# Cross attention with q, k and v of 512 tokens by seven products of quadrants, and a feature-major output

## The chip, the cores and the metric

The kernel runs on one core of one Trainium2 chip. A core has a matrix engine (TensorE, "PE" in the profile, with its weight loads shown apart as "PEld"), a vector engine (VectorE, "DVE"), a scalar engine (ScalarE, "ACT"), a general engine (GpSimd, "POOL") and a sync engine ("SP") that issues transfers. Matrix products are written to PSUM, eight banks of 128 partitions x 512 float32 values, and have to be copied from there to SBUF, the working memory of 128 partitions, before PE can use them again. The metric is the time of one execution on the device, in microseconds (us); smaller is better.

## What is computed

The program is a decoder of two layers with six sublayers; each adds its result to the tokens x (8 batches of 256 tokens, 512 features, float32) and normalizes. The change is in the fifth, the cross attention of the second layer. The context and the projected tokens themselves serve together as keys and values:

```python
q = jnp.einsum('bsd,ed->bse', x, wq)
k_new = jnp.einsum('bsd,ed->bse', x, wk)
v_new = jnp.einsum('bsd,ed->bse', x, wv)
k = jnp.concatenate([k_cache, k_new], axis=1)
v = jnp.concatenate([v_cache, v_new], axis=1)
scores = jnp.einsum('bqd,bkd->bqk', q, k) * (1.0 / math.sqrt(512))
attn = jax.nn.softmax(scores, axis=-1)
out = jnp.einsum('bqk,bkd->bqd', attn, v)
return jnp.einsum('bqd,ed->bqe', out, wo)
...
x = _layernorm(x + _L1_xattn_ref(x, mask, ctx_2048, ctx_2048, wq, wk, wv, wo), axis=-1)
```

k_cache and v_cache are both the context (256 tokens per batch), so each of the 256 queries of a batch has 512 keys, in one head of 512 features. The mask isn't applied by this function.

## The kernel before

The 2048 tokens are 16 tiles x[t] of 128 tokens (partitions) by 512 features. A group is 4 tiles, or 512 tokens, or two batches; there are NG = 4 groups. The contraction over 512 features is done in KB = 4 blocks of 128 partitions, so `project` (L192) issues four matmuls into one PSUM bank.

The stages around this one, self attention ahead of it and the routed attention behind it, have their order on PE, DVE, ACT and POOL written out by hand (`causal_attention`, `tc.manual_schedule`). The cross attention between them has not: the framework's scheduler takes the instructions in the order of the code as their priority, and puts a later one that is ready where an earlier one would wait. It also inserts all waits. A tile with `bufs=1` has a single buffer, and its next use waits until the last reader of the old one is done.

For each group (L1592 to L1605):

- SP issues the loads of the context token-major (`cx`, L1594) and feature-major (`ctxT`, L1596), 1 MB each, with two buffers each.
- `group_xT` turns the four tiles of x on PE (`transpose`, L185: four 128x128 transposes into one of two "tr" banks), and `evacuate` (L136) copies them to `xT`, in turn on ACT and DVE.
- `feature_major` (L1472) makes q and k with the features on partitions: for each of four feature blocks four matmuls of 512 columns into the one "mm" bank, then a copy. For q the copy multiplies by -1/sqrt(512) on ACT (L1482); for k it goes to ACT and DVE in turn.
- `token_major` (L1485) makes v with the tokens on partitions, in four such products.
- `Pipeline` (L269) runs three stages of each tile, shifted against each other: `scores` (matmuls of 256 columns against `ctxT` and against `kT`, a minimum on DVE, the exponential on ACT with the row sum, its reciprocal), `products` (the weights turned, 128 x 512 of attention output `po` in four matmuls, divided by the row sum on DVE into y, L1583) and `out_project` (L247: y turned, multiplied by wo, added to x and normalized; the normalization uses POOL for the reciprocal root, L164 and L165). `pipe.flush()` (L1599) finishes the tiles of the group before, between q and k.

The eight PSUM banks are: one for "mm" (products of q, k, v and output), two for transposes, two for `po`, three for scores (`attention_pools`, L1429). The weights wq, wk, wv, wo lie in `w_l1x`; they were loaded during the self attention, from 1301.3 to 1419.1 us.

Of the kernel before, what the change touches and what calls it, by code (L numbers as in the profile page):

```python
# [25 lines left out]
GT = TPG * P  # L30
KB = D // P
# [19 lines left out]
def decoder_kernel(ctx: ExitStack, tc: tile.TileContext, a: dict, out: bass.AP):  # L51
    nc = tc.nc
    xin = a["x"].rearrange("b s d -> (b s) d").rearrange("(t p) d -> p t d", p=P)
    cin = a["ctx_2048"].rearrange("b s d -> (b s) d").rearrange("(t p) d -> p t d", p=P)
# [3 lines left out]
    small = ctx.enter_context(tc.tile_pool(name="small", bufs=4))  # L58
# [5 lines left out]
    x = []  # L64
# [3 lines left out]
    def load_x(tiles):  # L68
# [13 lines left out]
        out=hide_b,  # L82
        in_=hide_b,
# [35 lines left out]
    ctx_d = dram.tile([P, KB, B * S], F32, tag="ctx_d", name="ctx_d")  # L119
# [16 lines left out]
    def evacuate(dst, src):  # L136

        flip[0] ^= 1
        if flip[0]:
            nc.scalar.copy(dst, src)  # L140
        else:
            nc.vector.tensor_copy(dst, src)
# [39 lines left out]
    def layernorm(dst, src):  # L182
        norm_later(dst, src)()

    def transpose(psum, dst, src):  # L185

        pt = psum.tile([P, KB, P], F32, tag="tr", name="pt")
        for k in range(KB):
            nc.tensor.transpose(pt[:, k, :], src[:, k * P : (k + 1) * P], ident)
        evacuate(dst, pt)  # L190

    def project(ps, lhsT, rhs, n=KB):  # L192

        for k in range(n):
            nc.tensor.matmul(ps, lhsT=lhsT(k), rhs=rhs(k), start=(k == 0), stop=(k == n - 1))  # L195
# [33 lines left out]

        return xT, [(0, [(TR, lambda ti=ti: step(ti))]) for ti in range(TPG)]  # L230

    def group_xT(work, psum, g):
        xT = work.tile([P, KB, GT], F32, tag="xT", name="xT", bufs=1)
        for ti in range(TPG):
            transpose(psum, xT[:, :, ti * P : (ti + 1) * P], x[g * TPG + ti])
        return xT
# [7 lines left out]
    def add_norm(work, t, ps):  # L244
        add_norm_later(work, t, ps)()

    def out_project(work, psum, t, y, w):  # L247

        yT = work.tile([P, KB, P], F32, tag="yT", name="yT")
        transpose(psum, yT, y)  # L250
        ps = psum.tile([P, D], F32, tag="mm", name="ps_o")
        project(ps, lambda k: yT[:, k, :], lambda k: w[:, k, :])
        add_norm(work, t, ps)

    def softmax_rows(ps, sc, nk, mn, sm):

        nc.vector.tensor_tensor_reduce(
            out=sc,
            in0=ps,
            in1=mask[:, 2 * P - nk :],  # L260
            scale=1.0,
            scalar=3.0e38,
            op0=ALU.add,
            op1=ALU.min,
            accum_out=mn,
        )
        nc.scalar.activation(sc, sc, AF.Exp, bias=mn, scale=-1.0, accum_out=sm)

    class Pipeline:  # L269

# [1155 lines left out]
                fill(9.0)  # L1426
                happen("end")

    def attention_pools(st, name):  # L1429
        work = st.enter_context(tc.tile_pool(name=f"{name}_work", bufs=2))  # L1430
        psum = st.enter_context(tc.tile_pool(name=f"{name}_ps", bufs=1, space=PSUM))
        ps_s = st.enter_context(tc.tile_pool(name=f"{name}_pss", bufs=3, space=PSUM))
        ps_t = st.enter_context(tc.tile_pool(name=f"{name}_pst", bufs=2, space=PSUM))

        class pools:
            @staticmethod
            def tile(shape, dt, tag, name):
                if tag == "tr":
                    return ps_t.tile(shape, dt, tag=tag, name=name)
                return psum.tile(shape, dt, tag=tag, name=name, bufs=2 if tag == "pv" else 1)  # L1440

        return work, pools, ps_s, ps_t
# [20 lines left out]
    def out_block(pools, yT, i, w, done):  # L1463
# [4 lines left out]
            lambda k: w[:, k, :],  # L1468
            done,
        )  # L1470

    def feature_major(work, pools, xT, w, at, tag, scale=None, bufs=2):  # L1472

        r = work.tile([P, KB, GT], F32, tag=tag, name=tag, bufs=bufs)
        for c in range(KB):
            cs = slice(at + c * P, at + (c + 1) * P)
            ps = pools.tile([P, GT], F32, tag="mm", name="ps_f")
            project(ps, lambda k: w[:, k, cs], lambda k: xT[:, k, :])
            if scale is None:
                evacuate(r[:, c, :], ps)  # L1480
            else:
                nc.scalar.mul(r[:, c, :], ps, scale)  # L1482
        return r

    def token_major(pools, xT, w, at, ti):  # L1485

        ps = pools.tile([P, D], F32, tag="mm", name="ps_t")
        project(
            ps, lambda k: xT[:, k, ti * P : (ti + 1) * P], lambda k: w[:, k, at : at + D]
        )  # L1490
        return ps

    def self_weights(w, behind):
        return load_w(w, 0, a["L1_attn_w_qkv"], 3 * D, behind), load_w(
# [55 lines left out]
    def cross_weights(w):  # L1550
# [2 lines left out]
            for i, n in enumerate(("wq", "wk", "wv", "wo"))  # L1553
        ]

    def cross_attention(wq, wk, wv, wo):
        def cross_step(work, pools, ps_s, g, ti, qT, kT, v, cx, ctxT):
            k0 = (ti // 2) * S
            sc = work.tile([P, 2 * S], F32, tag="sc", name="sc_x")
            sm = small.tile([P, 1], F32, tag="xsm", name="xsm")  # L1560

            def scores():
                ps = ps_s.tile([P, 2 * S], F32, tag="sc", name="ps_x")
                q = lambda k: qT[:, k, ti * P : (ti + 1) * P]
                project(ps[:, :S], q, lambda k: ctxT[:, k, k0 : k0 + S])
                project(ps[:, S:], q, lambda k: kT[:, k, k0 : k0 + S])
                mn = small.tile([P, 1], F32, tag="xmn", name="xmn")
                nc.vector.tensor_reduce(mn, ps, AX.X, ALU.min)
                nc.scalar.activation(sc, ps, AF.Exp, bias=mn, scale=-1.0, accum_out=sm)
                nc.vector.reciprocal(sm, sm)  # L1570

            def products():
                pT = work.tile([P, KB, P], F32, tag="pT", name="pT_x")
                transpose(pools, pT, sc)
                po = pools.tile([P, D], F32, tag="pv", name="po_x")
                t0 = (ti // 2) * 2
                project(
                    po,
                    lambda k: pT[:, k, :],
                    lambda k: cx[:, t0 + k, :] if k < 2 else v[:, t0 + k - 2, :],  # L1580
                )
                y = work.tile([P, D], F32, tag="row", name="y_x", bufs=3)
                nc.vector.tensor_scalar(y, po, sm, None, ALU.mult)  # L1583
                out.append(y)

            out = []
            return scores, products, lambda: out_project(work, pools, g * TPG + ti, out[0], wo)

        with ExitStack() as st:
            work, pools, ps_s, ps_t = attention_pools(st, "x")  # L1590
            pipe = Pipeline()
            for g in range(NG):  # L1592
                cx = work.tile([P, TPG, D], F32, tag="cx", name="cx_x")
# [10 lines left out]
                for ti in range(TPG):  # L1604
# [115 lines left out]
    with ExitStack() as st_self:  # L1720
# [6 lines left out]
        w = pool.tile([P, 2 * half], F32, tag="w", name="w_l1a")  # L1727
        with ExitStack() as st_blocks:
# [4 lines left out]
            ps_t = st_blocks.enter_context(tc.tile_pool(name="c_pst", bufs=2, space=PSUM))  # L1733
# [98 lines left out]
```

## Time and profile before

| what | value |
|---|---|
| median of 3 runs | 2313.8 us (2313.7 to 2317.38) |
| profiled execution | 2321.55 us, span 2319.8 us |
| PE busy over the span | 2148.9 us (93%) |
| DVE busy | 1194.6 us (51%) |
| POOL busy | 658.8 us (28%) |
| ACT busy | 424.1 us (18%) |
| cross attention, on PE | 1574.72 to 1951.72 us |

In the profile a row of a group gives the line, the engine, the operation, what it writes and reads by the program's names, shapes and count, then the busy time in us and the mean of one in ns, and then the idle time of the engine just before these instructions with what ended most of it. L195 is the line of the helper `project`; groups are therefore told apart by the tile that they write: `ps_f` is q and k, `ps_t` v, `ps_x` the scores, `po_x` the attention output, `ps_o` the output projection, `pt` a transpose. A row of the timeline gives start and length in us, then the same names; what stands in brackets is the idle time before it and what it waited for. Matmuls are pipelined and overlap, so their durations are longer than their distance from start to start.

### The profile page before, as it was taken

How to read it: one execution, taken by the hardware profiler on the slowest of the kernel's cores; microseconds unless marked ns; L12 is line 12 of the kernel's file. 1: busy time of each engine (PE TensorE's matmuls, PEld its weight loads, DVE VectorE, ACT ScalarE, POOL GpSimd, SP SyncE). 2: the span in 40 equal slices, each digit the busy share in tenths (PEclk: the TensorE clock that was granted, in tenths of full speed). 3: DMA queues.
4: the chain of work that ended last, by engine and by line, in shares of the span. 5: the costliest groups of instructions: out<-in, count | busy, mean ns of one | idle time of the engine just before them, and what ended most of it. 6: DMA issues, size and time to landing. Idle time of an engine off the chain costs nothing.

```text
span 2319.8 us, 35250 instructions
## 1 busy us (share of the span) xinstructions
PE 2148.9 (93%) x15064; PEld 1164.0 (50%) x15064; DVE 1194.6 (51%) x1847; ACT 424.1 (18%) x607; POOL 658.8 (28%) x768
## 2 busy tenths in 40 slices
PE   7799989888998998999969999999999999999996
PEld 4455555544444454555524455444554545555543
DVE  3566666657888963122224646451222213567667
ACT  1223233330000012211112222221111111112212
POOL 0344555455555723000022433230000000022223
PEclk9899999999999998999979999999999999999998
DMA  7899602305224143131140201003001000000000
GB/s 233 302 384 383 243 2 65 112 1 172 73 66 151 42 141 129 62 136 64 46 146 19 74 15 60 1 1 127 27 10 36 1 0 1 1 10 11 10 19 28
DMA packets 107851, 197.53 MB, mean 85 GB/s; under 512 B 6960, under 2 KB 26544, under 8 KB 107696
## 3 DMA queue, kind: packets, MB, share of 16 engines
q1 hardware_dynamic: 102576, 178.49, 22.1%
q0 software_dynamic: 5120, 16.78, 2.1%
q8 instruction: 121, 1.98, 0.3%
q14 instruction: 34, 0.28, 0.0%
HBM read 93.54 MB, written 112.20 MB: 89 GB/s over the span
## 4 chain that ended last, share of the span: by engine, by line
PE 40%; DVE 5%; POOL 2%; ACT 1%; issue 1%; DMA 1%; POOLq 0%; ACTq 0%; DVEq 0%
PE ps_f L206 7%; PE ps_t L206 6%; PE ps_f L195 5%; PE ps_t L195 2%; PE po_x L195 2%; PE ps_o L206 2%; PE ps_o L195 2%; PE ps_q L1203 2%; PE ps_x L195 2%; PE ps_k L1257 2%; PE ps_pv L1300 2%; PE ps_pv L1310 1%; DVE rsum L1318 1%; DVE neg L1210 1%; DVE bn_st L169 1%; PE ps_q L1193 1%
## 5 line engine op out<-in xcount | busy, mean ns | idle before, releaser
L1210 DVE TENSOR_REDUCE neg<-ps_q 128x12 f32<-128x1536 f32 x128 | 224.9, 1757 | 344.7 <-PE ps_q L1203 343.9
L195 PE MATMUL ps_y<-kv,wt 128*128 128x512 f32 x640 | 282.5, 600 | 5.5 <-POOL kv L563 3.8
L1275 POOL TENSOR_SCALAR_AFFINE_SELECT pT<-pT 128x1024 f32<-128x1024 f32 x128 | 140.1, 1095 | 514.3 <-ACT pT L1274 513.7
L1274 ACT ACTIVATE pT<-ps_k 128x1536 f32<-128x1536 f32 x128 | 185.6, 1450 | 539.1 <-PE ps_k L1266 517.4
L1318 DVE RECIPROCAL rsum<-ps_pv 128x256 f32<-128x256 f32 x128 | 224.1, 1751 | 42.1 <-PE ps_pv L1310 41.4
L195 PEld LDWEIGHTS ps_y<-kv,wt 128*128 128x128 f32 x640 | 120.8, 192 | 155.7 <-issue 137.5
L164 POOL TENSOR_SCALAR rstd<-bn_mv 128x1 f32<-128x1 f32 x80 | 16.6, 207 | 563.9 <-DVE bn_mv L170 559.9
L1285 POOL TENSOR_TENSOR pT<-pT 128x512 f32<-128x512 f32 x112 | 142.3, 1271 | 9.3
L195 PE MATMUL ps_f<-xT,w_l1x 128*128 128x512 f32 x256 | 120.1, 612 | 3.3 <-ACT qT L1482 2.1
L206 PE MATMUL ps_f<-xT,w_l1a 128*128 128x512 f32 x256 | 119.6, 611 | 3.0 <-ACT xT L219 3.0
L206 PE MATMUL ps_t<-w_l1f,xT 128*128 128x512 f32 x256 | 120.1, 607 | 0.3 <-DVE sel L1649 0.3
L1036 PE MATMUL po_m<-dn,hT 128*128 (+1 forms) x216 | 104.5, 622 | 11.8 <-ACT hT L1029 10.3
L1121 POOL DMA_INDIRECT w_l1x<-ys,slots x32 | 32.3, 1011 | 280.1 <-DMA ys<-y_m 272.3
L1310 PE MATMUL ps_pv<-pT,ones_v 128*32 128x256 f32 (+1 forms) x1152 | 86.2, 382 | 12.5 <-POOL pT L1285 10.4
L601 DVE TENSOR_REDUCE yc<-z 128x64 f32<-128x512 f32 x128 | 86.1, 674 | 6.2 <-issue 5.8
L1193 PEld LDWEIGHTS <-ident_b 128*128 128x128 bf16 x512 | 50.5, 99 | 75.7 <-issue 72.0
L1193 PE MATMUL ps_q<-hide_b,ident_b 128*128 128x256 bf16 x512 | 78.2, 276 | 9.7 <-ACT pT L1274 8.7
L195 PEld LDWEIGHTS ps_f<-xT,w_l1x 128*128 128x128 f32 x256 | 46.8, 193 | 62.3 <-issue 48.5
L1257 PE MATMUL ps_k<-qT,kz 32*128 32x256 f32 (+1 forms) x1024 | 69.5, 358 | 8.3 <-DVE neg L1210 6.7
L206 PEld LDWEIGHTS ps_f<-xT,w_l1a 128*128 128x128 f32 x256 | 46.9, 192 | 59.0 <-issue 54.2
L195 PE MATMUL pg<-gu,xT_b 128*128 x216 | 72.1, 470 | 1.4 <-ACT xT_b L219 1.4
L1018 DVE TENSOR_TENSOR h_b<-h_b,pg 128x352 f32<-128x352 f32 x36 | 18.8, 521 | 103.7 <-ACT h_b L1017 103.7
(304 smaller groups left out, 3511.6 us busy)
## 6 DMA issues: line engine op xcount, KB each, us to landing
xs<-zero SPq DMA_DIRECT2D x8, 4352.0 KB
ys<-zero SPq DMA_DIRECT2D x8, 4352.0 KB
filters<-in_L_xattn_k SPq DMA_DIRECT2D x4, 2560.0 KB
first_h<-xs SPq DMA_DIRECT2D x36, 256.0 KB
ys<-y_m SPq DMA_DIRECT2D x36, 256.0 KB
gu<-in_L_ffn_gate_up_proj SPq DMA_DIRECT2D x3, 2816.0 KB
wt<-filters SPq DMA_DIRECT2D x32, 256.0 KB
x<-in_x SPq DMA_DIRECT2D x16, 256.0 KB
```

The costliest lines, as they stand in the source:

```text
L195: nc.tensor.matmul(ps, lhsT=lhsT(k), rhs=rhs(k), start=(k == 0), stop=(k == n - 1))
L206: nc.tensor.matmul(ps[0], lhsT=lhsT(k), rhs=rhs(k), start=(k == 0), stop=(k == KB - 1))
L601: nc.vector.tensor_reduce(yc[:, lb], z, AX.X, ALU.add)
L1036: nc.tensor.matmul(po, lhsT=hT[:m, i, :], rhs=dn[i][:m, bass.ds(e, 1), :], start=(i == 0), stop=(i == len(FCH) - 1),)
L1193: nc.tensor.matmul(block[:, s, 0:3:2, :], lhsT=ident_b, rhs=hide_b.unsqueeze(1).broadcast_to([P, 2, P]), start=True, stop=False,)
L1210: nc.vector.tensor_reduce(neg[(u // upb) % 2][:, :, :, c].rearrange("p j s -> p s j"), block, AX.X, ALU.max, negate=True,)
L1257: nc.tensor.matmul(block[:, s, at, :], lhsT=k(rows, c, b * S + j * P, P), rhs=q(rows, c, b * S + j * P, P * (2 - j)), start=True, stop=False,)
L1274: nc.scalar.activation(p[:, 0:3].rearrange("p j s q -> p s j q"), block, AF.Exp)
L1275: nc.gpsimd.affine_select(out=p[:, 0:2].rearrange("p j s q -> p (j s) q"), in_=p[:, 0:2].rearrange("p j s q -> p (j s) q"), compare_op=ALU ...
L1285: nc.gpsimd.tensor_tensor(p[:, 3], p[:, 1], p[:, 2], ALU.add)
L1310: nc.tensor.matmul(ps[32 * s : 32 * s + 32, 1, j * P :], lhsT=ones_v, rhs=p[:, 1, s, :] if j else first[:, :, s, :], start=(j == 0), stop= ...
L1318: nc.vector.reciprocal(r, ps[:, 1, :])
```

## The change

It rewrites the cross attention; the other stages stay as they are.

- The three products of a group with wq, wk and wv are taken as products of 2 x 2 quadrants. `seven_weights` makes, once, three sums of quadrants of each weight matrix into new tiles and one in place (a21), on DVE for wq and on POOL for wk and wv. `seven_tokens` makes four differences of quadrants of `xT` per group, three on DVE and one on POOL. `seven_products` makes seven products of quadrants (each 256 x 256 x 256, in one bank), copies the first with ACT, and adds the others up on DVE straight from PSUM: seven additions, into the quadrants of q, k or v and into two partial sums u2 and u3 that have one buffer each, as p1 has.
- Scores are taken per batch (two tiles). The scale 1/sqrt(512) is no longer in q: it is in the exponential and, by a small DVE instruction, in the negated maximum.
- The attention output is computed with features on partitions, for a batch of 256 tokens at a time, so it needs no turning before the output projection. ACT copies it to `yT`. The division by the row sum moves into the residual: one `scalar_tensor_tensor` multiplies by the reciprocal and adds x.
- The context is loaded per batch (512 KB each), still with two buffers.
- PSUM is divided anew: four banks for "mm" (products, all transposes, output projection), two for `po`, two for scores. `xT`, `qT`, `kT`, `v`, `pT`, `yT` and the differences have one buffer each.
- Helpers that nothing else uses are removed; `transpose` gets the name of the bank's tag as a parameter.

```diff
+    def quadrants(m):
+
+        return [[m[:, 2 * j : 2 * j + 2, i * S : (i + 1) * S] for j in range(2)] for i in range(2)]
+
+    def seven_weights(work, w, eng):
+
+        (a11, a12), (a21, a22) = quadrants(w)
+        sums = [work.tile([P, 2, S], F32, tag="ws", name="ws", bufs=9) for _ in range(3)]
+        eng.tensor_tensor(sums[0], a21, a22, ALU.add)
+        eng.tensor_tensor(sums[1], sums[0], a11, ALU.subtract)
+        eng.tensor_tensor(sums[2], a12, sums[1], ALU.subtract)
+        eng.tensor_tensor(a21, a11, a21, ALU.subtract)
+        return a11, a12, sums[1], a21, a22, sums[0], sums[2]
+
+    def seven_tokens(work, xT):
+
+        (b11, b21), (b12, b22) = quadrants(xT)
+        t = work.tile([P, 4, 2, S], F32, tag="ts", name="ts", bufs=1)
+        nc.vector.tensor_tensor(t[:, 0], b12, b11, ALU.subtract)
+        nc.gpsimd.tensor_tensor(t[:, 2], b22, b12, ALU.subtract)
+        nc.vector.tensor_tensor(t[:, 1], b22, t[:, 0], ALU.subtract)
+        nc.vector.tensor_tensor(t[:, 3], b21, t[:, 1], ALU.subtract)
+        return b11, b21, t[:, 1], t[:, 2], t[:, 3], t[:, 0], b22
+
+    def seven_products(work, pools, weights, tokens, dst, token_major=False):
+
+
+
+        def product(n):
+            ps = pools.tile([P, 2, S], F32, tag="mm", name="ps_7")
+            rows, cols = (tokens, weights) if token_major else (weights, tokens)
+            for i in range(2):
+                project(
+                    ps[:, i, :],
+                    lambda k: rows[n][:, k, i * P : (i + 1) * P],
+                    lambda k: cols[n][:, k, :],
+                    n=2,
+                )
+            return ps
+
+        def part(name):
+            return work.tile([P, 2, S], F32, tag=name, name=name, bufs=1)
+
+        p1, u2, u3 = part("p1"), part("u2"), part("u3")
+        add = lambda out, ps, other: nc.vector.tensor_tensor(out, ps, other, ALU.add)
+        nc.scalar.copy(p1, product(0))
+        add(dst(0, 0), product(1), p1)
+        add(u2, product(2), p1)
+        add(u3, product(3), u2)
+        add(dst(1, 0), product(4), u3)
+        ps = product(5)
+        add(dst(1, 1), ps, u3)
+        add(u2, ps, u2)
+        add(dst(0, 1), product(6), u2)
+
     def cross_attention(wq, wk, wv, wo):
-        def cross_step(work, pools, ps_s, g, ti, qT, kT, v, cx, ctxT):
-            k0 = (ti // 2) * S
-            sc = work.tile([P, 2 * S], F32, tag="sc", name="sc_x")
-            sm = small.tile([P, 1], F32, tag="xsm", name="xsm")
+        scale = D**-0.5
+
+        def batch(work, pools, ps_s, n, qT, kT, v, cx, ctxT):
+
+            q0 = n % 2 * S
+            sc, sm = [], []
 
             def scores():
-                ps = ps_s.tile([P, 2 * S], F32, tag="sc", name="ps_x")
-                q = lambda k: qT[:, k, ti * P : (ti + 1) * P]
-                project(ps[:, :S], q, lambda k: ctxT[:, k, k0 : k0 + S])
-                project(ps[:, S:], q, lambda k: kT[:, k, k0 : k0 + S])
-                mn = small.tile([P, 1], F32, tag="xmn", name="xmn")
-                nc.vector.tensor_reduce(mn, ps, AX.X, ALU.min)
-                nc.scalar.activation(sc, ps, AF.Exp, bias=mn, scale=-1.0, accum_out=sm)
-                nc.vector.reciprocal(sm, sm)
+                for i in range(2):
+                    ps = ps_s.tile([P, 2 * S], F32, tag="sc", name="ps_x")
+                    q = lambda k: qT[:, k, q0 + i * P : q0 + (i + 1) * P]
+                    project(ps[:, :S], q, lambda k: ctxT[:, k, :])
+                    project(ps[:, S:], q, lambda k: kT[:, k, q0 : q0 + S])
+                    mx = small.tile([P, 1], F32, tag="xmx", name="xmx")
+                    nc.vector.tensor_reduce(mx, ps, AX.X, ALU.max, negate=True)
+                    nc.vector.tensor_scalar(mx, mx, scale, None, ALU.mult)
+                    sc.append(work.tile([P, 2 * S], F32, tag="sc", name="sc_x"))
+                    sm.append(small.tile([P, 1], F32, tag="xsm", name="xsm"))
+                    nc.scalar.activation(sc[i], ps, AF.Exp, bias=mx, scale=scale, accum_out=sm[i])
+                    nc.vector.reciprocal(sm[i], sm[i])
 
             def products():
-                pT = work.tile([P, KB, P], F32, tag="pT", name="pT_x")
-                transpose(pools, pT, sc)
-                po = pools.tile([P, D], F32, tag="pv", name="po_x")
-                t0 = (ti // 2) * 2
-                project(
-                    po,
-                    lambda k: pT[:, k, :],
-                    lambda k: cx[:, t0 + k, :] if k < 2 else v[:, t0 + k - 2, :],
-                )
-                y = work.tile([P, D], F32, tag="row", name="y_x", bufs=3)
-                nc.vector.tensor_scalar(y, po, sm, None, ALU.mult)
-                out.append(y)
-
-            out = []
-            return scores, products, lambda: out_project(work, pools, g * TPG + ti, out[0], wo)
+                pT = work.tile([P, KB, S], F32, tag="pT", name="pT_x", bufs=1)
+                for i in range(2):
+                    transpose(pools, pT[:, :, i * P : (i + 1) * P], sc[i], "mm")
+                yT.append(work.tile([P, KB, S], F32, tag="yT", name="yT_x", bufs=1))
+                for f in range(0, KB, 2):
+                    po = pools.tile([P, 2, S], F32, tag="pv", name="po_x", bufs=2)
+                    for i in range(2):
+                        cols = slice((f + i) * P, (f + i + 1) * P)
+                        project(
+                            po[:, i, :],
+                            lambda k: cx[:, k, cols] if k < 2 else v[:, q0 // P + k - 2, cols],
+                            lambda k: pT[:, k, :],
+                        )
+                    nc.scalar.copy(yT[0][:, f : f + 2, :], po)
+
+            def out():
+                for i in range(2):
+                    ps = pools.tile([P, D], F32, tag="mm", name="ps_o")
+                    project(
+                        ps, lambda k: yT[0][:, k, i * P : (i + 1) * P], lambda k: wo[:, k, :]
+                    )
+
+                    t = 2 * n + i
+                    r = work.tile([P, D], F32, tag="row", name="res")
+                    nc.vector.scalar_tensor_tensor(r, ps, sm[i], x[t], ALU.mult, ALU.add)
+                    layernorm(x[t], r)
+
+            yT = []
+            return scores, products, out
 
         with ExitStack() as st:
-            work, pools, ps_s, ps_t = attention_pools(st, "x")
+            work = st.enter_context(tc.tile_pool(name="x_work", bufs=2))
+            pools = st.enter_context(tc.tile_pool(name="x_ps", bufs=4, space=PSUM))
+            ps_s = st.enter_context(tc.tile_pool(name="x_pss", bufs=2, space=PSUM))
+            wq7 = seven_weights(work, wq, nc.vector)
+            wk7 = seven_weights(work, wk, nc.gpsimd)
+            wv7 = seven_weights(work, wv, nc.gpsimd)
             pipe = Pipeline()
             for g in range(NG):
-                cx = work.tile([P, TPG, D], F32, tag="cx", name="cx_x")
-                nc.sync.dma_start(out=cx, in_=cin[:, g * TPG : (g + 1) * TPG, :])
-                ctxT = work.tile([P, KB, GT], F32, tag="ctxT", name="ctxT_x")
-                nc.sync.dma_start(out=ctxT, in_=ctx_d[:, :, g * GT : (g + 1) * GT])
-                xT = group_xT(work, pools, g)
-                qT = feature_major(work, pools, xT, wq, 0, "qT", -(D**-0.5))
+                ctxs = []
+                for n in range(2 * g, 2 * g + 2):
+                    cx = work.tile([P, 2, D], F32, tag="cx", name="cx_x")
+                    nc.sync.dma_start(out=cx, in_=cin[:, 2 * n : 2 * n + 2, :])
+                    ctxT = work.tile([P, KB, S], F32, tag="ctxT", name="ctxT_x")
+                    nc.sync.dma_start(out=ctxT, in_=ctx_d[:, :, n * S : (n + 1) * S])
+                    ctxs.append((cx, ctxT))
+                xT = work.tile([P, KB, GT], F32, tag="xT", name="xT", bufs=1)
+                for ti in range(TPG):
+                    transpose(pools, xT[:, :, ti * P : (ti + 1) * P], x[g * TPG + ti], "mm")
+                x7 = seven_tokens(work, xT)
+                qT = work.tile([P, KB, GT], F32, tag="qT", name="qT", bufs=1)
+                q = quadrants(qT)
+                seven_products(work, pools, wq7, x7, lambda i, l: q[l][i])
                 pipe.flush()
-                kT = feature_major(work, pools, xT, wk, 0, "kT", bufs=1)
+                kT = work.tile([P, KB, GT], F32, tag="kT", name="kT", bufs=1)
+                k = quadrants(kT)
+                seven_products(work, pools, wk7, x7, lambda i, l: k[l][i])
                 v = work.tile([P, TPG, D], F32, tag="v", name="v_x", bufs=1)
-                for ti in range(TPG):
-                    evacuate(v[:, ti, :], token_major(pools, xT, wv, 0, ti))
-                for ti in range(TPG):
-                    pipe.push(*cross_step(work, pools, ps_s, g, ti, qT, kT, v, cx, ctxT))
+                vq = quadrants(v)
+                seven_products(work, pools, wv7, x7, lambda i, l: vq[i][l], True)
+                for n, (cx, ctxT) in zip(range(2 * g, 2 * g + 2), ctxs):
+                    pipe.push(*batch(work, pools, ps_s, n, qT, kT, v, cx, ctxT))
             pipe.flush()
 
 
```

More of the change, by code (lines that the diff above doesn't have):

```diff
@@ L183, in layernorm, with transpose @@
         norm_later(dst, src)()
-    def transpose(psum, dst, src):
-        pt = psum.tile([P, KB, P], F32, tag="tr", name="pt")
+    def transpose(psum, dst, src, tag="tr"):
+        pt = psum.tile([P, KB, P], F32, tag=tag, name="pt")
         for k in range(KB):
@@ L230, in turned_group @@
         return xT, [(0, [(TR, lambda ti=ti: step(ti))]) for ti in range(TPG)]
-    def group_xT(work, psum, g):
-        xT = work.tile([P, KB, GT], F32, tag="xT", name="xT", bufs=1)
-        for ti in range(TPG):
-            transpose(psum, xT[:, :, ti * P : (ti + 1) * P], x[g * TPG + ti])
-        return xT
     def add_norm_later(work, t, ps):
@@ L242, in add_norm_later @@
         return norm_later(x[t], r)
[L244 to L265, printed above, removed]
-        )
-        nc.scalar.activation(sc, sc, AF.Exp, bias=mn, scale=-1.0, accum_out=sm)
     class Pipeline:
@@ L1427, in causal_attention @@
                 happen("end")
[L1429 to L1442, printed above, removed]
     def feature_block(pools, r, xT, w, at, c, scale=1.0):
@@ L1470, in out_block @@
         )
[L1472 to L1487, printed above, removed]
-        project(
-            ps, lambda k: xT[:, k, ti * P : (ti + 1) * P], lambda k: w[:, k, at : at + D]
-        )
-        return ps
     def self_weights(w, behind):
@@ L1556, in cross_attention @@
     def cross_attention(wq, wk, wv, wo):
-        def cross_step(work, pools, ps_s, g, ti, qT, kT, v, cx, ctxT):
-            k0 = (ti // 2) * S
-            sc = work.tile([P, 2 * S], F32, tag="sc", name="sc_x")
-            sm = small.tile([P, 1], F32, tag="xsm", name="xsm")
+        scale = D**-0.5
+        def batch(work, pools, ps_s, n, qT, kT, v, cx, ctxT):
+            q0 = n % 2 * S
+            sc, sm = [], []
             def scores():
-                ps = ps_s.tile([P, 2 * S], F32, tag="sc", name="ps_x")
-                q = lambda k: qT[:, k, ti * P : (ti + 1) * P]
-                project(ps[:, :S], q, lambda k: ctxT[:, k, k0 : k0 + S])
-                project(ps[:, S:], q, lambda k: kT[:, k, k0 : k0 + S])
-                mn = small.tile([P, 1], F32, tag="xmn", name="xmn")
-                nc.vector.tensor_reduce(mn, ps, AX.X, ALU.min)
-                nc.scalar.activation(sc, ps, AF.Exp, bias=mn, scale=-1.0, accum_out=sm)
-                nc.vector.reciprocal(sm, sm)
-            def products():
-                pT = work.tile([P, KB, P], F32, tag="pT", name="pT_x")
-                transpose(pools, pT, sc)
-                po = pools.tile([P, D], F32, tag="pv", name="po_x")
-                t0 = (ti // 2) * 2
-                project(
-                    po,
-                    lambda k: pT[:, k, :],
-                    lambda k: cx[:, t0 + k, :] if k < 2 else v[:, t0 + k - 2, :],
-                )
-                y = work.tile([P, D], F32, tag="row", name="y_x", bufs=3)
-                nc.vector.tensor_scalar(y, po, sm, None, ALU.mult)
-                out.append(y)
-            out = []
-            return scores, products, lambda: out_project(work, pools, g * TPG + ti, out[0], wo)
@@ L1601, in cross_attention @@
+                k = quadrants(kT)
+                seven_products(work, pools, wk7, x7, lambda i, l: k[l][i])
                 v = work.tile([P, TPG, D], F32, tag="v", name="v_x", bufs=1)
-                for ti in range(TPG):
-                    evacuate(v[:, ti, :], token_major(pools, xT, wv, 0, ti))
-                for ti in range(TPG):
-                    pipe.push(*cross_step(work, pools, ps_s, g, ti, qT, kT, v, cx, ctxT))
+                vq = quadrants(v)
+                seven_products(work, pools, wv7, x7, lambda i, l: vq[i][l], True)
```

## The prediction

> **What bounds the kernel now.** I read the page's busy shares first (PE 93%, DVE 51%), then the stage the change touches. On PE's timeline the cross attention runs from its first transpose at 1574.72 us to 1951.72 us, where the next stage's first transpose starts: 377.0 us. The busy time by stretch (columns: length, PE, PEld, DVE, ACT, POOL busy with counts, granted clock, DMA share, GB/s) splits it at the end of the first group's query products:
>
> ```profile
> 1574.70:1599.30 24.60, 19.67 (x48) 9.06 (x49) 2.80 (x5) 2.96 (x5) 0.74 (x2) 0.86 0.83 300
> 1599.30:1951.70 352.40, 344.12 (x1041) 179.56 (x1040) 80.51 (x146) 41.35 (x83) 11.09 (x30) 1.00 0.04 12
> ```
>
> PE is full for 352 us at clock 1.00; DVE has 23%, ACT 12%, POOL 3%. So work taken off PE here shortens the stage, and DVE and ACT have room. What PE does, from the groups of this stage:
>
> ```profile
> L195 PE MATMUL ps_f<-xT,w_l1x 128*128 128x512 f32 x256 | 120.1, 612 | 3.3 <-ACT qT L1482 2.1 <-issue 0.8
> L195 PE MATMUL ps_t<-w_l1x,xT 128*128 128x512 f32 x128 | 59.0, 604 | 0.0
> L195 PE MATMUL ps_o<-w_l1x,yT 128*128 128x512 f32 x128 | 57.6, 593 | 0.9 <-DVE yT L142 0.9
> L195 PE MATMUL ps_x<-ctxT_x,qT 128*128 128x256 f32 x128 | 32.7, 379 | 0.0
> ...
> L195 PE MATMUL po_x<-cx_x,pT_x 128*128 128x512 f32 x64 | 31.6, 601 | 4.3 <-DVE pT_x L142 4.3
> ...
> L189 PE MATMUL pt<-ident,y_x 128*128 128x128 f32 x64 | 9.6, 273 | 0.0
> ```
>
> The trace records two matmuls for each one the code issues (four contraction blocks give x8). Durations include the pipeline's tail, so I take the distance from start to start, from PE's timeline:
>
> ```profile
> 1587.01 3.70 PE L195 MATMUL ps_f<-xT,w_l1x 128*128 128x512 f32 x8 [0.69 <-ACT qT L1482]
> 1591.39 3.70 PE L195 MATMUL ps_f<-xT,w_l1x 128*128 128x512 f32 x8 [0.69 <-ACT qT L1482]
> ...
> 1730.59 1.89 PE L195 MATMUL ps_x<-ctxT_x,qT 128*128 128x256 f32 x8
> 1732.31 1.89 PE L195 MATMUL ps_x<-kT,qT 128*128 128x256 f32 x8
> 1734.04 0.60 PE L189 MATMUL pt<-ident,sc_x 128*128 128x128 f32 x4
> ...
> 1755.74 1.09 PE L189 MATMUL pt<-ident,x 128*128 128x128 f32 x8 [0.51 <-DVE xT L142]
> ```
>
> Sixteen 256-column matmuls take 1734.04 - 1730.59 = 3.45 us, 0.2156 each. An unbroken output projection (1647.24 to 1650.67, eight matmuls) gives 0.429 per 512 columns, and four transposes take 0.435 (0.109 each). The first two lines show what the single product bank costs where nothing fills the wait: 4.38 us apart instead of 3.43.
>
> **PE's own work, before.** 512 columns: 256 + 128 + 128 (ps_f, ps_t, ps_o) and 128 (po_x) = 640 x 0.429 = 274.6. Scores: 256 x 0.2156 = 55.2. Transposes of x, sc_x and y_x: 192 x 0.109 = 20.9. Sum 350.7, so 26.3 of the 377.0 us is loss. Of it, 9.1 lies before 1599.3 (first transposes and four query products are 15.5 us of work in 24.6: late first copy, a cold clock, three waits of 0.95) and 17.2 after.
>
> **PE's own work, after.** Each of q, k, v of a group becomes seven products of 2 halves x 2 contraction blocks x 2 records = 8 matmuls of 256 columns; 12 x 7 x 8 = 672. The attention output is now 8 batches x 4 feature blocks x 8 = 256 matmuls of 256 columns instead of 128 of 512: no gain. Scores 256 stay. So 1184 x 0.2156 = 255.3; output projection 128 x 0.429 = 54.9; transposes 128 x 0.109 = 14.0 (the 64 of y_x go). Sum 324.2: **26.5 us less**, 19.9 from the products, 7.0 from y_x, minus 0.3 for the two rates.
>
> Here a rule speaks against the change. The Trainium skill (TensorE: Matmul & The Clock Gate, Back-to-back issue gap) says that in a stream of load-and-matmul pairs both set the spacing, 81 ns at 128 columns and 131 at 512. Interpolated, 256 columns would cost about 1.5 times their share of a 512, and my 928 new 256-column matmuls 928 x 0.1 = some 95 us more: slower than before. The trace has the row itself: 0.2156 against 0.429 / 2 = 0.2145, with loads of 0.190 beneath. I take the row; the margin under the load is only 0.025 us each.
>
> **Evictions.** Removed from DVE: eight copies each of kT and v (11.0), y_x scaling (12.0), yT copies (2.7), four pT copies that move to ACT (2.7). Added: per product set one ACT copy and seven adds that read PSUM; nearest row res<-ps_o,x at 0.692: 84 x 0.69 = 58.0. Token differences 12 x 0.69 = 8.3, weight sums 2.8, scaling the maximum 16 x 0.16 (row of xsm) = 2.6, the fused residual 16 x 0.06 = 1.0 (scalar_tensor_tensor 0.75 at L1130 against 0.69). DVE goes from 83 to about 128 of 344 us, ACT from 44 to 37. A product takes PE 1.72 us and its DVE add 0.69, and four banks instead of one stand between them, so I cost the adds at nothing on the path; without that cover each is worth up to the 0.95 seen above. The scale on the maximum sits in front of the exponent, hidden by the other tile's scores (3.45 us).
>
> **The start of the stage.** PE cannot multiply before tiles 0 and 1 of x are turned and copied, and DVE copies tile 1. The new weight sums come earlier in DVE's order, and POOL gets eight more:
>
> ```profile
> 1576.55 0.55 DVE L178 TENSOR_SCALAR x<-res,bn_mv,rstd 128x512 f32<-128x512 f32 x1 [0.95 <-POOL rstd L165]
> 1577.19 0.58 ACT L140 COPY xT<-pt 128x512 f32<-128x512 f32 x1 [13.62 <-DVE x L178]
> ...
> 1580.53 5.79 PE L195 MATMUL ps_f<-xT,w_l1x 128*128 128x512 f32 x8 [0.83 <-issue]
> ```
>
> DVE is free at 1577.1. What two-input operations cost beside POOL is seen in the long convolution:
>
> ```profile
> 600.96 0.72 DVE L563 TENSOR_TENSOR kv<-first_h 128x512 f32<-128x512 f32 x1
> ...
> 604.86 1.06 POOL L563 TENSOR_TENSOR kv<-first_h 128x512 f32<-128x512 f32 x1
> 605.42 1.05 DVE L563 TENSOR_TENSOR kv<-first_h 128x512 f32<-128x512 f32 x1
> ```
>
> The second DVE row ends 0.55 after POOL's. Its line's median is 0.835. The Trainium skill (SBUF — State Buffer, Who interferes with whom) says a VectorE instruction with two SBUF inputs and a GpSimd one that reads SBUF exclude each other whole. By the median, four sums take 3.3 us and the first product starts at about 1581.1, 0.6 late. By the rule, with POOL busy back to back (1.27 each, row L1285), they alternate: 4 x (1.27 + 0.55) = 7.3, then the copy's 0.69: 1585.3, 4.8 late. The two sums differ by 4 us. I take the rule, because row 605.42 does exactly that. POOL's ninth operation (the third product's token difference for group 0) is done near 1592.7, about when PE has finished three products at the cold clock. Against this stand the three query waits of 0.95 that more banks remove: +4.8 - 2.85 = **+1.95 us**. Bounds: -2.85 (no exclusion) to +7 (DVE behind all eight POOL operations). In later groups three DVE differences and one on POOL lie beside two products (3.4 us) and the flushed batch.
>
> **The other waits.** Of a steady group's 4.15 us loss (query products start at 1665.61, 1757.56, 1849.52: 91.95 apart for 87.7 of work), the turning of x with two banks takes 1.24 and goes with four; 1.4 are waits for pT copies and stay, since 256-column products need both tiles' copies; the rest, the single product bank, goes. Three groups x 1.4 plus the 4.6 of the last part: **9 us instead of 17.2**. Bounds 3 (scheduler finds filling everywhere) and 17.2.
>
> **Moved transfers.** SP now issues 16 loads of 512 KB in place of 8 of 1 MB, in the same order, two batches ahead. No instruction waited for ctxT_x before; the second batch's load stands behind the previous group's products in SP's queue, and k and v (24 us) lie ahead of its use. Nothing on the path; uncovered, a megabyte at the 300 GB/s shown costs 3.5 us per group.
>
> **Sum.** 324.2 + 9.1 + 1.95 + 9 = 344.3, against 377.0: 32.7 less. The span 2319.8 becomes 2287.1 and that execution's 2321.55 becomes 2288.9. The median of the runs is 2313.8, 7.75 below the profiled one, a third of a per cent; the saving carries over whole: **2281 us**.
>
> **Rivals.** (1) The waits stay: only the arithmetic comes, less the latest start: 377.0 - 26.5 + 7 = 357.5 gives 2294, and 2298 if the single copies add 1 us a group. For it: single-copy tiles xT, qT, yT, pT and one set of partial sums. Against: the banks and the filling PE already finds. (2) Slower, by the rate: long runs of 256 columns do not keep 0.2156. Place: 928 new matmuls; it decides from 32.7 / 928 = 0.035 us each; at the skill's 0.1 the time is about 2374. Against: sixteen in a row at full rate. (3) PE waits for the adds, since each partial sum is built on the one before: 84 x 0.95 = 80 gives 2361; it cancels the gain from 0.39 us per product. Against: DVE at 37% and four banks.
>
> **How the numbers follow.** As summed, 0.70, own range 2274 to 2289; rival 1, 0.20; rivals 2 and 3 at full or part strength 0.08; 0.02 for a cancellation. Low end: best gaps and start, 324.2 + 6.25 + 3 = 333.5, gives 2270; with the rates' rounding 2268. High end 2298, that of rival 1. Faster by over 0.2% (4.6 us, about what can be told) 0.92, within 0.2% 0.02, slower 0.06.
>
> **What would show it.** Product matmuls x672 at 0.216 apart; first product near 1585; DVE sums stretched to about 1.8 while POOL runs; stage about 344 us; DVE near 37%. Wrong if PE's idle time names the adds, if product matmuls are farther apart than 0.23, or if group distances stay above 88.

## The result, and the profile after

The changed kernel takes **2275.6 us** (median of 4 runs, 2272.8 to 2280.68) against 2315.59 us of the kernel before beside it (2313.7 to 2319.4): 40.0 us less, ratio **0.9828** with a 95% interval of 0.9804 to 0.9852. Forecast were 2281 us, 32.7 us less, in a range of 2268 to 2298.

To compare kernels whose stages begin at different moments I measure the stage from the last normalization of the self attention to the last one of the cross attention, both on DVE: 1576.55 to 1954.50 before, 1570.08 to 1909.85 after. That is 377.95 and **339.8 us**, 38.2 less. On PE, counted as in the prediction (first transpose at 1568.24, the next stage's at 1908.01), the stage after is 339.8 us too, against 344.3 forecast and 377.0 before. The profiled span shrank by 44.1 us; the other 6 lie ahead of the stage, whose start falls anywhere from 1570 to 1581 us in the nine kernels profiled here, with the same code ahead of it. So the stage's own length is the finer measure. It still differs by 2.6 us between two profiles of the changed kernel (the last experiment), so a smaller difference between two single profiles says nothing.

The busy time by stretch of the changed kernel, columns as before, split where the first group's query products end:

```profile
1568.00:1591.00 23.00, 16.84 (x72) 14.09 (x73) 15.57 (x19) 1.66 (x3) 14.92 (x11) 0.85 0.64 230
1591.00:1908.00 317.00, 314.39 (x1370) 249.57 (x1368) 120.21 (x211) 34.49 (x73) 16.42 (x33) 1.00 0.07 21
```

PE is still what is full: 314.4 of 317 us. DVE has risen from 23% to 38%, ACT fell from 12% to 11%. Groups of the stage:

```profile
L194 PE MATMUL ps_o<-w_l1x,yT_x 128*128 128x512 f32 x128 | 57.3, 595 | 0.7 <-ACT yT_x L1579 0.7
...
L194 PE MATMUL ps<-ts,ws 128*128 128x256 f32 x128 | 32.4, 398 | 4.0 <-DVE ts L1508 4.0
...
L1532 DVE TENSOR_TENSOR u<-ps,u 128x512 f32<-128x512 f32 x24 | 16.5, 686 | 13.3 <-PE ps L194 13.3
```

The products (`ps`) stand under several names of operands, 672 matmuls in all. Before the 128 of `ps<-ts,ws`, PE waited 4.0 us for a token difference. These are all of PE's waits that the trace lists from the stage's start to the next stage's first transpose (columns: who for whom, us in total, times, longest):

```profile
PE ps L194 <- DVE ts L1508: 4.0, 1, 4.0
PE ps L194 <- ACT xT L139: 1.9, 1, 1.9
PE pt L217 <- DVE res L1590: 0.8, 1, 0.8
PE pt L188 <- DVE res L234: 0.8, 1, 0.8
PE ps_o L194 <- ACT yT_x L1579: 0.7, 1, 0.7
PE po_x L194 <- ACT pT_x L139: 0.6, 3, 0.2
PE pt L188 <- ACT sc_x L1562: 0.5, 1, 0.5
```

None is for an addition (L1532). It is the other way round: the additions wait for PE, and take 0.69 us each as estimated. The rate, from PE's timeline over a whole set of products, here those of v:

```profile
1603.28 3.62 PE L194 MATMUL ps<-w_l1x,xT 128*128 128x256 f32 x16
1606.73 1.89 PE L194 MATMUL ps<-ws,ts 128*128 128x256 f32 x8
1608.46 3.62 PE L194 MATMUL ps<-w_l1x,ts 128*128 128x256 f32 x16
1611.91 1.89 PE L194 MATMUL ps<-ws,ts 128*128 128x256 f32 x8
1613.64 1.89 PE L194 MATMUL ps<-ws,xT 128*128 128x256 f32 x8
1615.36 0.81 PE L194 MATMUL ps_x<-ctxT_x,qT 128*128 128x256 f32 x3
```

56 matmuls in 1615.36 - 1603.28 = 12.08 us, 0.2157 each, with nothing between them. The start of the stage, from the timeline of all engines:

```profile
1571.33 0.68 DVE L141 COPY xT<-pt 128x512 f32<-128x512 f32 x1
...
1572.11 3.69 PE L194 MATMUL ps<-xT,w_l1x 128*128 128x256 f32 x16 [1.90 <-ACT xT L139]
1572.61 1.59 POOL L1497 TENSOR_TENSOR ws<-ws,w_l1x 128x512 f32<-128x512 f32 x1
1573.01 1.75 DVE L1499 TENSOR_TENSOR w_l1x<-w_l1x 128x512 f32<-128x512 f32 x1
...
1574.17 1.71 POOL L1499 TENSOR_TENSOR w_l1x<-w_l1x 128x512 f32<-128x512 f32 x1
1574.68 1.75 DVE L1498 TENSOR_TENSOR ws<-w_l1x,ws 128x512 f32<-128x512 f32 x1
...
1578.13 1.63 DVE L1508 TENSOR_TENSOR ts<-xT,ts 128x512 f32<-128x512 f32 x1
...
1579.82 3.78 PE L194 MATMUL ps<-ts,ws 128*128 128x256 f32 x8 [4.02 <-DVE ts L1508]
...
1583.40 4.50 PE L194 MATMUL ps<-ts,w_l1x 128*128 128x256 f32 x16
...
1583.76 1.27 POOL L1498 TENSOR_TENSOR ws<-w_l1x,ws 128x512 f32<-128x512 f32 x1
```

DVE's sums and POOL's go in step, a pair in about 1.67 us from start to start. Alone, a DVE sum starts 0.60 us after the one before it (shown in a later experiment), and POOL's last one, with DVE's sums over, takes 1.27. PE ends its first two products at 1575.8 and has to wait for the second difference until 1579.8. From 1580 to 1584 the granted clock (the share of its full speed that PE may run at, the third column from the end) is 0.50:

```profile
1580.00:1584.00 4.00, 4.00 (x10) 3.19 (x11) 1.81 (x3) 0.00 (x0) 4.00 (x4) 0.50 0.77 265
```

So the next eight matmuls take 3.6 us instead of 1.7, and the sixteen after them 4.3 instead of 3.45.

### The profile page after: what moved, and what is told of

Read it like the earlier page. It is cut to its first block, busy times and chain, and to the rows that moved or that the text cites. A ratio compares the mean times of both kernels' runs of the same rounds, so it can differ in the third digit from the quotient of the medians.

```text
span 2275.7 us, 36145 instructions
## 1 busy us (share of the span) xinstructions
PE 2110.2 (93%) x15416; PEld 1236.4 (54%) x15416; DVE 1245.9 (55%) x1923; ACT 415.9 (18%) x595; POOL 679.2 (30%) x780
## 5 line engine op out<-in xcount | busy, mean ns | idle before, releaser
L1089 POOL DMA_INDIRECT w_l1x<-ys,slots x32 | 32.7, 1022 | 279.0 <-DMA ys<-y_m 271.1
L205 PEld LDWEIGHTS ps_t<-w_l1f,xT 128*128 128x128 f32 x256 | 45.5, 189 | 52.2 <-issue 50.5
L1268 PE MATMUL ps_pv<-pT,v 128*32 128x256 f32 (+1 forms) x1024 | 56.3, 338 | 18.0 <-POOL pT L1243 16.8
L1225 PE MATMUL ps_k<-qT,kT 32*128 32x256 f32 (+1 forms) x1024 | 68.5, 354 | 3.8 <-ACT pT L1242 2.7
```

The source lines that it names most:

```text
L205: nc.tensor.matmul(ps[0], lhsT=lhsT(k), rhs=rhs(k), start=(k == 0), stop=(k == KB - 1))
L1225: nc.tensor.matmul(block[:, s, at, :], lhsT=k(rows, c, b * S + j * P, P), rhs=q(rows, c, b * S + j * P, P * (2 - j)), start=True, stop=False,)
```

## The experiments

The questions: how much of the 38 us is arithmetic, how much the banks; what hides the additions; whether POOL makes the wait at the start. Stage times below are from DVE's normalizations, as above. Each experiment's runs stood beside runs of the kernel before.

**Only the banks, in the kernel before.**

```diff
-                if tag == "tr":
-                    return ps_t.tile(shape, dt, tag=tag, name=name)
-                return psum.tile(shape, dt, tag=tag, name=name, bufs=2 if tag == "pv" else 1)
+                if tag == "pv":
+                    return psum.tile(shape, dt, tag=tag, name=name, bufs=2)
+                return psum.tile(shape, dt, tag="mm", name=name, bufs=4)
```

with two banks of scores in place of three.

> The kernel before with nothing changed but its eight PSUM banks in the cross attention: four for the products of q, k, v, all transposes and the output projection, two for the attention output, two for scores (before: one, two of transposes, two, three). Theory A, that the single product bank and the two transpose banks made most of the 26.3 us by which PE's stage exceeded its work: PE's own work stays 350.7 us, the three query waits of 0.95 and about 10 of the later 17.2 us go, so the stage on PE falls from 377.0 to 362 to 367 us and the time by 10 to 15 us. Rival B, that those waits come from the dependences of the pipeline and not from the banks: less than 4 us.

Measured: 2304.65 us against 2319.25, ratio 0.993 (0.9907 to 0.9953); stage 365.3 us, 12.7 less. Theory A holds. PE's largest waits in the stage, first of the kernel before, then of this one:

```profile
PE po_x L195 <- DVE pT_x L142: 4.3, 5, 1.0
PE pt L189 <- DVE xT L142: 2.6, 6, 0.5
PE ps_f L195 <- ACT qT L1482: 2.1, 3, 0.7
```

```profile
PE po_x L195 <- DVE pT_x L142: 4.3, 5, 1.0
PE ps_f L195 <- DVE bn_mv L170: 2.7, 3, 0.9
PE ps_f L195 <- ACT xT L140: 1.9, 1, 1.9
```

The waits for the copy of a query product and for a second pair of transposes are gone; the wait for the turned weights (pT) is untouched by more banks. In their place stand three waits of 0.9 us for the copy of the last tile of x (the first time it ends at 1658.27, and PE starts at 1658.41; the trace names the DVE instruction after it, which ends at 1658.36). So the listed waits fall little. More went in two other ways. In the kernel before most products started about 0.1 us late even where the wait for their bank was filled, which comes to 7 us over the stage, here to 2. And over the first 15 us of the stage the granted clock was 0.77 in the kernel before's trace and 1.00 in this one; some 3 us of the 12.7 are that, and no run here shows whether the banks brought it.

**Plain products for q, k and v, the rest as changed.**

```diff
-                seven_products(work, pools, wq7, x7, lambda i, l: q[l][i])
+                plain(pools, qT, wq, xT)
...
+    def plain(pools, dst, rows, cols):
+        for c in range(KB):
+            ps = pools.tile([P, GT], F32, tag="mm", name="ps_f")
+            project(ps, lambda k: rows[:, k, c * P : (c + 1) * P], lambda k: cols[:, k, :])
+            evacuate(dst[:, c, :], ps)
```

> The changed kernel with q, k and v as plain products of 512 columns again (copied by ACT and DVE in turn), all else as changed: feature-major output, division in the residual, four banks. Theory A, that the products bring their count of matmuls and nothing is lost to their additions: PE's work is 324.2 + 19.9 = 344.1 us, but the wait of 4.0 us and the cold clock after it (about 2.8) at the start of the stage go with the sums, so the stage is about 353 us against 339.8 and the time some 13 us above the changed kernel. Rival B, that the additions cost time on the path: less than 8 us above it, or none.

Measured: 2294.44 us, ratio to the kernel before 0.9884 (0.9854 to 0.9914); stage 355.8 us. So the seven products are worth 16.0 us of stage out of 19.9 us of matmuls. In time this kernel is 24.8 us below the kernel before, and the changed kernel 40.0 and, run again, 44.5 below the runs beside it, so they are worth 15 to 20 us. That is on theory A's side, above its 13.

Where the missing 4 us went can be read from the distance between groups, taken from the first normalization of a group to that of the next. It falls from 88.15 us to 82.17 in the changed kernel, by 5.98, which is about the 4.97 of matmuls per group and a wait of 0.9 that plain products have for the copy of the group's last tile. So in later groups nothing is lost to the additions. But up to the first group's first normalization the gain is 0.75 us, where the matmuls give 6.6: there lie the wait of 4.0 us and 2.7 us lost at a half clock that this trace does not have (its granted clock over the first 15 us of the stage is 1.00).

With the first experiment the whole splits: banks 12.7, all that lies between (the feature-major output, the division in the residual, and the scale and the loads that moved) 365.3 - 355.8 = 9.5, seven products 16.0. Each is the difference of two single profiles and carries their 2 to 3 us. The middle part is more than the 7.0 us of transposes; the pT waits went with it, from 4.3 us to the 0.6 in the list above.

**One bank for products, transposes and output projection.**

```diff
-            pools = st.enter_context(tc.tile_pool(name="x_ps", bufs=4, space=PSUM))
+            pools = st.enter_context(tc.tile_pool(name="x_ps", bufs=1, space=PSUM))
```

> The changed kernel with one bank instead of four for products, transposes and output projection. Theory A, that four banks are what hides the additions: each of the 84 products, 32 transposed tiles and 16 output projections has to wait for its copy or addition, up to 0.95 us each where no score or attention output fills in: 132 x 0.95 = 125 us at most, and with about half of it filled 50 to 80 us more than the changed kernel, so slower than the kernel before. Rival B, that PE finds enough other work: less than 15 us more.

Measured: 2391.43 us, ratio 1.0312 (1.0284 to 1.0341): slower than the kernel before by 72 us. Stage 448.9 us, 109 more than with four banks. Theory A's mechanism holds, but 109 is more than its middle guess of 50 to 80. PE's waits:

```profile
PE ps_o L194 <- DVE res L1590: 9.6, 12, 0.9
...
PE ps L194 <- DVE qT L1532: 7.3, 9, 0.9
...
PE ps L194 <- ACT p L1533: 5.7, 8, 0.7
```

Here the additions and copies that no wait named in the changed kernel are on the path, up to 0.9 us each. Over the stage PE's granted clock is 0.93, against 1.00 in all but the start of the changed kernel's. How the 109 us split comes out of the starts of all matmuls of the stage and the trace's record of the clock: waits cost 87 us against 10 in the changed kernel, matmuls at half clock lost 24 against 3, and late starts of up to 0.15 us each 13 against 3. So the waits alone, 77 us more, are within the guess, and some 50 of the 125 us were filled; the clock and the late starts were in neither theory.

**Two banks**, the same line with `bufs=2`.

> The changed kernel with two banks instead of four for products, transposes and output projection. Theory A, what matters is that one product is computed while the one before is added up: a product takes PE 1.72 us and its addition 0.69 and some latency, so two banks hide nearly all, and the stage is 340 to 350 us against 339.8 with four and about 450 with one. Rival B, that four banks are needed because the product used twice, the first copy on ACT and other work in DVE's queue delay the release: 360 us or more.

Measured: 2284.38 us, ratio 0.9848 (0.9817 to 0.9879); stage 343.9 us. Theory A: two banks hide all but 4 to 7 us (the changed kernel's two profiles have 339.8 and 337.2), so most of the cover is the second bank. The times can't show the rest: this ratio's interval overlaps the changed kernel's. But the distance between groups does, and PE's waits tell what is no longer covered:

```profile
PE pt L188 <- DVE pT_x L141: 2.4, 3, 0.8
PE pt L188 <- DVE xT L141: 1.1, 3, 0.4
...
PE ps L194 <- DVE qT L1532: 0.3, 1, 0.3
```

It is the copies of transposes; of the 84 additions only one is waited for, 0.3 us. The distances between groups of these kernels, which do not contain the start of the stage:

| kernel | us from group to group |
|---|---|
| before | 91.96 |
| only the banks, in the kernel before | 90.37 |
| plain products, the rest as changed | 88.15 |
| changed | 82.17 |
| changed, two banks | 83.73 |
| changed, one bank | 108.5 and 110.5 |

**The weight sums of wk and wv on DVE instead of POOL.**

```diff
-            wk7 = seven_weights(work, wk, nc.gpsimd)
-            wv7 = seven_weights(work, wv, nc.gpsimd)
...
                 x7 = seven_tokens(work, xT)
+                if g == 0:
+                    wk7 = seven_weights(work, wk, nc.vector)
+                    wv7 = seven_weights(work, wv, nc.vector)
```

> The changed kernel with the eight weight sums of wk and wv on DVE, behind the first group's token differences in the code, instead of on POOL; PE's order is the same. Theory A, that POOL's operations stretched DVE's by shutting them out: DVE's sums take 0.6 to 0.7 us each in a row instead of 1.1 to 1.75, PE's wait ahead of the third query product falls from 4.0 us to 1 to 2 us and the cold clock behind it mostly goes: the stage falls from 339.8 to 334 to 337 us, the time by 3 to 6 us. Rival B, that the wait comes from the number of operations in DVE's order: the wait stays above 3 us, since DVE now has two more operations in front of the second difference.

Measured: 2274.83 us, ratio 0.9799 (0.977 to 0.9827); stage 337.0 us, at theory A's edge. But the changed kernel's second profile has 337.2, and the intervals of its ratios (0.9804 to 0.9852 and, run again, 0.9793 to 0.9837) overlap this one, so neither the stage nor the time shows a gain. What the trace shows is the exclusion. DVE's and POOL's rows:

```profile
1578.03 0.68 DVE L1499 TENSOR_TENSOR w_l1x<-w_l1x 128x512 f32<-128x512 f32 x1
1578.63 0.68 DVE L1498 TENSOR_TENSOR ws<-w_l1x,ws 128x512 f32<-128x512 f32 x1
...
1580.05 1.58 POOL L1507 TENSOR_TENSOR ts<-xT 128x512 f32<-128x512 f32 x1 [4.51 <-DVE xT L141]
1580.43 1.75 DVE L1506 TENSOR_TENSOR ts<-xT 128x512 f32<-128x512 f32 x1
1582.11 0.68 DVE L1497 TENSOR_TENSOR ws<-ws,w_l1x 128x512 f32<-128x512 f32 x1
```

The same two sums that took 1.75 us take 0.68 with POOL silent, and the only long DVE row is the one beside POOL's only remaining operation. PE's wait for the second difference is 2.14 us, above the 1 to 2 forecast, and the cold clock did not go: the eight matmuls behind it take 2.6 us instead of 1.7. That rival B is not wholly wrong shows in what is left: the scheduler put sums of wk in DVE's gaps, ahead of the second difference.

**All of them on DVE, those of wk and wv held behind the first group's differences**, and the changed kernel once more beside it.

```diff
-        nc.gpsimd.tensor_tensor(t[:, 2], b22, b12, ALU.subtract)
         nc.vector.tensor_tensor(t[:, 1], b22, t[:, 0], ALU.subtract)
-        nc.vector.tensor_tensor(t[:, 3], b21, t[:, 1], ALU.subtract)
+        nc.vector.tensor_tensor(t[:, 2], b22, b12, ALU.subtract)
+        last[:] = [nc.vector.tensor_tensor(t[:, 3], b21, t[:, 1], ALU.subtract)]
...
+        if behind:
+            wait_for(first.ins, behind, "behind the differences of the tokens")
```

> The changed kernel with every weight sum and token difference on DVE, and the eight sums of wk and wv held behind the first group's differences; POOL does none, PE's order is the same. Theory A, exclusion by POOL plus operations in front of the second difference make the whole wait at the start: DVE then has eight operations of about 0.6 us up to the second difference, 4.9 us from when it comes free, when PE ends its first two products too; the wait of 4.0 us (2.1 with the sums alone moved) falls below 0.6, PE's clock stays full behind it, and the stage falls from 339.8 to 332 to 334 us, the time by 5 to 8 us below the changed kernel's. Rival B, something else is late there (the weights' loads, PE's clock): the wait stays at 2 us or the clock cold, the stage above 336.

> The changed kernel itself once more, beside the others on one chip: 2270 to 2282 us, 34 to 45 us below the kernel before, its stage on PE 339 to 341 us.

Measured: 2276.96 us, ratio 0.9807 (0.9786 to 0.9828), stage 334.2; the changed kernel again 2277.09 us, ratio 0.9815 (0.9793 to 0.9837), stage 337.2. PE's timeline at the start:

```profile
1583.25 5.38 PE L194 MATMUL ps<-xT,w_l1x 128*128 128x256 f32 x16 [1.90 <-ACT xT L139]
1588.47 1.89 PE L194 MATMUL ps<-ts,ws 128*128 128x256 f32 x8
```

The wait is gone: the third product follows at once. The stage is 3.0 and 5.6 us shorter than in the changed kernel's two profiles; on PE the second of these has 337.2 us too, below the 339 to 341 expected. The expected 5 to 8 us in the time did not come: the medians differ by 0.13 us and the intervals overlap, so the time can't tell this kernel from the changed one. Part of why is the clock. The first two products ran at a granted 0.58 here (5.2 us instead of 3.45), where in the changed kernel's first profile they ran at 1.00 and its third at 0.50. In its second profile the first two were the cold ones as well, which left only 2.34 us to wait:

```profile
1572.00:1576.00 4.00, 3.63 (x10) 2.98 (x11) 4.00 (x4) 0.41 (x2) 3.92 (x3) 0.61 1.01 422
1576.00:1580.00 4.00, 1.75 (x8) 1.16 (x6) 3.86 (x5) 0.23 (x1) 4.00 (x4) 0.96 1.06 349
```

A cold clock at the start hides part of the wait. The pair to compare is therefore this kernel and that second profile, with the cold products at the same place: 3.0 us, from one pair.

## Why the prediction was right

**PE's own work.** Right. The trace shows the counts and the rate that the sum of 324.2 us rests on, and over 56 matmuls in a row, not only 16. Rival 2, the slower rate that the spacing rule quoted in the prediction would have brought (some 95 us), is out.

**Evictions at nothing on the path.** Right, and tested: with four banks no addition is waited for; with two one is, and the stage is 4 to 7 us longer, mostly by the copies of transposes (3.5 us of listed waits); with one bank it is 109 us longer. Rival 3's price of 0.95 is about that of a single eviction that nothing covers (0.7 to 0.9 us of idle time with one bank), but even there part of the 132 evictions was covered.

**The start.** The sum was 11.05 us of loss, measured are 9.1 (22.95 us from 1568.24 to 1591.19 for 16 transposes and 56 matmuls, 13.8 us of work). But its parts were wrong. "First product near 1585" put that product 10.6 us behind the first transpose; it began 3.9 us behind it, at 1572.1, since the scheduler put the copy of tile 1 behind one sum and not behind four. The exclusion is there as taken from the rule, DVE's sums stretched to 1.75 us, but it delays the third product instead of the first. The measured loss is 2.1 us up to the first product, 4.3 in front of the third and 2.7 at half clock behind it. That this comes within 2 us of the forecast is luck: a wait too many in one place stood for a wait too few in another.

**The other waits.** 9 us forecast; from 1591.19 to 1908.01 PE needs 316.8 us for 310.4 of work: 6.4. In this term the pT waits were mis-sized: they were to stay with 1.4 us a group, and are 0.6 in all, because the output projection and the next group's transposes fill them. Groups now start their queries 82.17 us apart (1639.29, 1721.46), for 81.05 of work.

**Moved transfers and the scale on the maximum.** No wait on them appears in the stage. Right as far as that shows.

So the arithmetic of 26.5 us was as counted; the rest of the stage's gain on PE, 11 us instead of 6, is PE's waits. Rival 1, that these stay, fell: in the kernel before, the new banks alone were worth 12.7. Two sums of the prediction are off by its own terms, without consequence: the first product comes to 1585.1 and not 1585.3, and a steady group's loss to 4.25 us and not 4.15. In the medians the gain is 40.0 us against 32.7; 4.5 of the difference is the stage on PE, and the rest lies within the 6 to 8 us over which each kernel's runs spread.

## What to carry to other kernels

Where PE is full, count matmuls by start-to-start distance and then ask what each product's copy hides behind: the second PSUM bank was worth some 105 us here, the third and fourth together 4 to 7, and about a third of the 38 us gained was to be had by dividing the banks anew without any new arithmetic. Seven products instead of eight paid because their additions fell to an engine with three quarters of its time free. Two-input additions shared between DVE and POOL are no way to go faster: a pair took 1.67 us in step where DVE alone does two in 1.2. Taking POOL out changed the time by less than these runs can tell, though.

## What the runs showed of the hardware

POOL suffers from the exclusion as well as DVE: 1.71 us for an operation that takes 1.27 alone, so the pair takes 1.67 us, a little less than the 1.82 summed from the rule. And the same code had its cold clock at different places of the same start, 1.00 then 0.50 in one profile, 0.61 then 0.96 in the other. With it differed the wait, by 1.7 us, and the stage, by 2.6 us, from one execution to the next. In the two experiments without seven products, after the same wait of 1.9 us ahead of the first product, the clock was 1.00 from the start.
